# Conditioned recurrence with residual on Trainium2: one product of half B's z moved between half A's products, and one update moved ahead of a transpose

## The chip, the cores and the metric

The kernel runs on one core of a Trainium2 chip. The metric is the device time of one execution in microseconds; the time before is the median of three runs, 1672.14 us (1670.59 to 1672.17).

## What is computed

A gated recurrence over 512 steps of a batch of 8, with 512 inputs and 512 hidden units, and the input added to its output. Cut to what matters:

```python
def step(h, x_t):
    fused = sigmoid(concatenate([x_t, h]) @ w_W + w_b)
    hidden_state, output_state = split(fused, 2)        # r and z below
    memory_state = x_t @ wx_W + wx_b + hidden_state * (h @ wh_W + wh_b)
    h_new = output_state * h + (1.0 - output_state) * tanh(memory_state)
    return h_new, h_new
return x + swapaxes(scan(step, cond, x_by_time), 0, 1)
```

Each step needs the state of the step before in full, so three products with h (for r, z and hh = h @ wh_W + wh_b) and all that follows them lie on a loop through the steps. The products with x do not depend on the state.

## The kernel before

**Layout.** The 512 hidden units are cut into four chunks of 128, the contraction rows of the products. Chunks 0 and 1 are half A of the state (tile `hT` for A, called hTA in the profile), chunks 2 and 3 are half B (hTB). The state is the stationary operand of each product, in 32 columns (8 batch entries for each of 4 steps in a group), and the weights stream past it. The array is used as four column strips of 32 (`128*32` in the profile): the index j of a product picks the strip, and output partitions 32j to 32j+31. In float32 each product shows in the profile as two weight loads and two matmuls, here called two passes.

**Banks.** The outputs of a step lie in three PSUM tiles: `A` (192 columns: hh, z and r of half A), `B` (128 columns: r and hh of half B) and `C` (64 columns: z of half B). There are two sets of them, used in turn by groups of four steps; the x products and biases are put there ahead of time by copies.

**Order on TensorE.** `ORDER` (line 26) is a string, and the loop of lines 349 to 358 issues it in every step but the first (which has `FIRST`). "B0" means: bank B, chunk 0, four products, one for each strip. So A0, A1, B0, B1, C0, C1 read half A's state and A2, A3, B2, B3, C2, C3 read half B's. Behind the twelve items come seven products of the x side for later groups (line 362); the strip of the first product rotates with `turn`, which grows by 7 a step. So three strips get two x products in a step and one gets one, each strip being the short one in every fourth step. The x side runs from step 5 on and issues 62 blocks of 56 products.

**Order on VectorE and ScalarE.** Lines 437 to 462, under a schedule written out by hand: the order of the calls is the order in each engine's queue. For half A: `turn_r(0)` transposes r out of its bank (tr) and ScalarE takes its sigmoid into `md0`; `turn_h(0)` transposes hh into `md1`; `turn_z(0)` transposes z (tz), followed by a sigmoid. `memory(0, q)` is a scan on VectorE that forms the memory state of chunk q, and a tanh on ScalarE. `update(0, q)` is a scan that writes chunk q of the new state of half A. For half B the same follows with index 1: tr, md1 and tz of B stand among the updates of A. Line 446 makes `update(0, 1)` wait for the sigmoid of r of B. Half B's memory scans and updates come last (lines 457 to 460), then two copies of the new state on ScalarE, and small work for later groups.

So A0 of the next step waits for `update(0, 0)`, A1 for `update(0, 1)`, A2 for `update(1, 0)` and A3 for `update(1, 1)`; the transposes of half A wait for the last product of bank A, which is A3's, the transposes tr and md1 of half B for B3, and tz of half B for C3.

Of the kernel before, what the change touches and what calls it, by code (L numbers as in the profile page):

```python
# [22 lines left out]
IDLE = 3  # L23
SYNC = mybir.DependencyInfo(mybir.DependencyClass.Sync, mybir.DependencyReason.DATA)

ORDER = "A0 B0 A1 A2 A3 B1 B2 B3 C0 C1 C2 C3"

FIRST = "A0 x A1 x A2 x A3 B0 B1 B2 B3 C0 C1 C2 C3"

# [11 lines left out]
def tile_cond_rnn_residual(  # L41
# [184 lines left out]
    def act(key, out_, in_, func, **kw):  # L226
        inst = nc.scalar.activation(out_, in_, func, **kw).ins  # L227
        if key in written:
            tc.declare_no_dep(inst, written[key], reason="ordered through VectorE")
        written[key] = inst  # L230
        return inst
# [108 lines left out]
    for i in range(T):  # L340
# [7 lines left out]

        for n in (ORDER if i else FIRST).split():
            if n == "x":  # L350
# [16 lines left out]
        def scan(c_, out_, d0, d1):  # L367

            return nc.vector.tensor_tensor_scan(  # L369
                *[t_[:, :, c_].rearrange("p n c s -> p (n c s)") for t_ in (out_, d0, d1)],  # L370
                0.0,
                ALU.mult,
                ALU.add,
            ).ins
# [8 lines left out]
        def turned(n, hf):  # L383
            t_ = work.tile([P, 2, 32], F32, tag=f"t{n}{hf}", name=f"t{n}{hf}_{i}")
            inst = nc.vector.transpose(t_.rearrange("p c n -> p (c n)"), raw[n][hf]).ins  # L385
            return t_[:, :, rows], inst
# [4 lines left out]
        def turn_r(hf):  # L391
            tr, _ = turned("r", hf)
            r_done[hf] = act(
                ("r", hf, g % 2, s),
                md0[hf][g % 2][:, rows, :, 1].rearrange("p n c -> p c n"),
                tr,
                AF.Sigmoid,
            )

        def turn_h(hf):  # L400
            inst = nc.vector.transpose(  # L401
                md1[hf][g % 2][:, :, :, 0].rearrange("p n c -> p c n"), raw["h"][hf]
            ).ins
            h_done[hf] = inst
            if hf == 0 and i + 1 - NH in pool_done:
                tc.add_manual_dep(inst, pool_done[i + 1 - NH].name, SYNC)

        def turn_z(hf):
            tz, _ = turned("z", hf)
            if hf == 0:  # L410
                inst = nc.vector.memset(idle[:, IDLE - 1 :], 0.0).ins
                tc.add_manual_dep(inst, h_done[0].name, SYNC)
            act(
                ("zc", hf, i % 2),
                hd0[hf][i % 2][:, :, :, 2].rearrange("p n c -> p c n"),
                tz,
                AF.Sigmoid,
                scale=-1.0,
            )
# [6 lines left out]
        def memory(hf, q):  # L426

            c_ = slice(q, q + 1)
            scan(c_, ms[hf], md0[hf][g % 2][:, rows], md1[hf][g % 2][:, rows])
            act(("n", hf, q, i % NH), state(hf, i, 1)[:, :, c_], ms[hf][:, :, c_, 1], AF.Tanh)  # L430

        def update(hf, q):
            s1 = (i + 1) % GS
            new = hT[hf][(i + 1) % NH][:, B * s1 : B * s1 + B]
            return scan(slice(q, q + 1), new, hd0[hf][i % 2], hT[hf][i % NH][:, rows])
# [4 lines left out]
        memory(0, 0)  # L440
        memory(0, 1)
        turn_r(1)
        turn_h(1)
        update(0, 0)
        turn_z(1)
        tc.add_manual_dep(update(0, 1), r_done[1].name, SYNC)
        if i == 0:
# [167 lines left out]
```

## Time and profile before

| what | value |
| --- | --- |
| median of three runs | 1672.14 us (1670.59 to 1672.17) |
| the profiled execution's own time | 1671.53 us |
| its span | 1669.5 us |
| granted TensorE clock | 0.999 |
| steps | 512 |
| busy: PE, weight loads, VectorE, ScalarE, GpSimd | 99%, 98%, 65%, 62%, 18% of the span |

How to read it: PE is TensorE's matmuls, PEld its weight loads, DVE is VectorE, ACT ScalarE, POOL GpSimd. A row of a timeline has the start and the duration in us, the engine, the line of the kernel, the operation, output<-inputs, and how many instructions are merged in it; a bracket gives the idle time of the engine ahead of it and what ended it. The duration of a matmul's record is that of one pass through the array; passes of one strip overlap in the pipeline, so the time from one start to the next is shorter than the duration. A row of the groups ends with busy us, mean ns of one, and the idle time ahead of it. The tile name hTA<-hd0A,hTA is an update of half A, m<-md0B,md1B a memory scan of half B, tr<-B the transpose of r of half B, md1B<-B that of hh, tz<-C that of z.

### The profile page before, as it was taken

What the parts mean: (1) busy time and instruction counts of PE and PEld (TensorE: products, weight loads), DVE (VectorE), ACT (ScalarE), POOL (GpSimd) and SP (SyncE); (2) the same over time, 40 slices, a digit from 0 to 9 for tenths busy, and PEclk for the clock granted to TensorE, in tenths of its full rate; (3) what the DMA queues carried; (4) which work ended last, traced back from release to release, by engine and by line L of the source; (5) the groups of instructions that cost most, each with busy time, mean ns of one, the idle gap of its engine ahead of it and who ended that gap; (6) DMA issues with size and microseconds to landing.
All of it is one profiled execution on the core that took longest, in us unless ns stands there. A gap on an engine that the chain in (4) does not pass through costs nothing.

```text
span 1669.5 us, 130236 instructions
## 1 busy us (share of the span) xinstructions
PE 1658.5 (99%) x56238; PEld 1639.1 (98%) x56238; DVE 1090.2 (65%) x9387; ACT 1029.7 (62%) x5822; POOL 301.7 (18%) x1281
## 2 busy tenths in 40 slices
PE   8999999999999999999999999999999999999998
PEld 5999999999999999999999999999999999999997
DVE  6666666666666666666666666666666666666666
ACT  3666666666666666666666666666666666666665
POOL 1111111111111111111111111111111111111111
PEclk9999999999999999999999999999999999999999
DMA  4000000000000000000000000000000000000000
GB/s 181 11 15 17 15 15 15 17 15 15 14 17 15 15 14 18 14 14 15 18 15 15 14 16 16 15 14 18 15 14 14 18 15 15 15 16 12 10 10 10
DMA packets 37304, 31.43 MB, mean 19 GB/s; under 512 B 4084, under 2 KB 35060, under 8 KB 36600
## 3 DMA queue, kind: packets, MB, share of 16 engines
q1 hardware_dynamic: 36576, 22.95, 4.4%
q8 instruction: 440, 7.21, 1.8%
q14 instruction: 136, 1.11, 0.2%
q10 hardware_dynamic: 152, 0.16, 0.0%
HBM read 14.70 MB, written 8.39 MB: 14 GB/s over the span
## 4 chain that ended last, share of the span: by engine, by line
PE 98%; DVE 1%; DMA 0%; issue 0%; ACT 0%
PE A L199 44%; PE B L199 23%; PE xp L199 20%; PE C L199 12%; DMA rows<-in_bias_dram 0%; DVE tr L385 0%; DVE m L369 0%; DVE tz L385 0%; DVE md1B L401 0%; DVE hTA L369 0%; DVE md1A L401 0%; DVE bias L214 0%; ACT hTB L227 0%; ACT xp L235 0%; DVE rows L131 0%
## 5 line engine op out<-in xcount | busy, mean ns | idle before, releaser
L199 PE MATMUL A<-wa,hTA 128*32 128x192 f32 x8176 | 639.0, 329 | 2.3 <-DVE hTA L369 2.3
L199 PE MATMUL B<-wb,hTA 128*32 128x128 f32 x8192 | 575.2, 273 | 0.0
L199 PE MATMUL A<-wa,hTB 128*32 128x192 f32 x8176 | 508.0, 326 | 0.4 <-DVE hTB L369 0.4
L199 PEld LDWEIGHTS B<-wb,hTA 128*32 128x32 f32 x8192 | 472.9, 122 | 1.1
L385 DVE STREAM_TRANSPOSE tr<-A 128x64 f32<-128x64 f32 x511 | 127.7, 250 | 462.5 <-PE A L199 462.5
L199 PE MATMUL B<-wb,hTB 128*32 128x128 f32 x8192 | 399.5, 273 | 0.0
L199 PEld LDWEIGHTS A<-wa,hTA 128*32 128x32 f32 x8176 | 386.8, 123 | 6.6 <-DVE hTA L369 4.0
L199 PEld LDWEIGHTS A<-wa,hTB 128*32 128x32 f32 x8176 | 373.6, 122 | 2.5 <-DVE hTB L369 0.8
L227 ACT ACTIVATE md0A<-tr 128x16 f32<-128x16 f32 x512 | 112.2, 219 | 419.9 <-DVE tr L385 419.9
L518 POOL TENSOR_TENSOR ot<-xin,hTB 128x16 f32<-128x16 f32 x503 | 125.9, 250 | 1323.4 <-DVE hTB L369 1312.9
L199 PEld LDWEIGHTS B<-wb,hTB 128*32 128x32 f32 x8192 | 322.3, 122 | 0.0
L199 PE MATMUL C<-wb,hTA 128*32 128x64 f32 x8192 | 290.2, 219 | 0.0
L199 PE MATMUL C<-wb,hTB 128*32 128x64 f32 x8192 | 289.7, 220 | 0.1
L199 PEld LDWEIGHTS C<-wb,hTA 128*32 128x32 f32 x8192 | 267.7, 122 | 0.0
L199 PE MATMUL xp<-tw,sx 128*32 128x192 f32 x2976 | 237.5, 326 | 0.0
L199 PEld LDWEIGHTS C<-wb,hTB 128*32 128x32 f32 x8192 | 229.8, 123 | 0.3 <-issue 0.3
L369 DVE TENSOR_TENSOR_SCAN hTB<-hd0B,hTB 128x24 f32<-128x24 f32 x1024 | 157.8, 196 | 100.9 <-ACT hTB L227 99.8
L369 DVE TENSOR_TENSOR_SCAN hTA<-hd0A,hTA 128x24 f32<-128x24 f32 x1024 | 191.9, 187 | 0.0
L199 PE MATMUL xp<-wx,xin 128*32 128x192 f32 (+1 forms) x2048 | 180.9, 331 | 0.0
L227 ACT ACTIVATE hd0B<-tz 128x16 f32<-128x16 f32 x512 | 115.2, 225 | 93.4 <-DVE tz L385 93.4
L227 ACT ACTIVATE hTB<-hTB 128x16 f32<-128x16 f32 x512 | 120.5, 235 | 79.8 <-DVE hTB L369 73.7
L227 ACT ACTIVATE hTB<-m 128x8 f32<-128x8 f32 x1024 | 160.6, 206 | 0.0
(92 smaller groups left out, 2491.0 us busy)
## 6 DMA issues: line engine op xcount, KB each, us to landing
out_dram<-ot SPq DMA_DIRECT2D x128, 64.0 KB, 2.0
xin<-in_x_dram SPq DMA_DIRECT2D x112, 64.0 KB, 2.5
wx<-in_wx_dram SPq DMA_DIRECT2D x4, 768.0 KB, 7.0
wa<-in_wa_dram SPq DMA_DIRECT2D x4, 384.0 KB, 8.9
wb<-in_wb_dram SPq DMA_DIRECT2D x1, 1152.0 KB
xin<-in_x_dram SPq DMA_DIRECT2D x3, 256.0 KB, 8.5
wb<-in_wb_dram SPq DMA_DIRECT2D x1, 384.0 KB, 10.9
head<-in_xh_dram ACTq DMA_DIRECT2D x1, 144.0 KB, 5.0
```

What stands on the lines that cost most here:

```text
L199: nc.tensor.matmul(out_, lhsT, rhs, start=start, stop=False, skip_group_check=True)
L227: inst = nc.scalar.activation(out_, in_, func, **kw).ins
L369: return nc.vector.tensor_tensor_scan(*[t_[:, :, c_].rearrange("p n c s -> p (n c s)") for t_ in (out_, d0, d1)], 0.0, ALU.mult, ALU.add,).ins
L385: inst = nc.vector.transpose(t_.rearrange("p c n -> p (c n)"), raw[n][hf]).ins
L518: return engine.tensor_tensor(ot[:, t, 2 * hf : 2 * hf + 2, :].rearrange("p c n -> p n c"), x_of(c, slice(2 * hf, 2 * hf + 2), t, 1).rearr ...
```

## The change

The order of the products in a step, and the place of one update in VectorE's order:

```diff
-ORDER = "A0 B0 A1 A2 A3 B1 B2 B3 C0 C1 C2 C3"
+ORDER = "A0 C0 A1 A2 A3 B0 B1 B2 B3 C1 C2 C3"
...
         memory(0, 0)
         memory(0, 1)
         turn_r(1)
+        update(0, 0)
         turn_h(1)
-        update(0, 0)
         turn_z(1)
         tc.add_manual_dep(update(0, 1), r_done[1].name, SYNC)
```

C0 (64 columns) takes the place of B0 (128 columns) between A0 and A1, and B0 goes behind A3, ahead of B1. On VectorE the first update of half A goes ahead of the transpose of hh of half B and stays behind the transpose of r of half B. `FIRST`, the order of step 0, stays as it is. Nothing is added and nothing is left out.

## The prediction, made before the change was run

> **What bounds the kernel now.** I read the page first, then the table of waits, then a row of the groups for the period, then one step's timelines on each engine. All times are us from the span's start. The page and its chain of waits:
>
> ```profile
> span 1669.5 us, 130236 instructions
> PE 1658.5 (99%) x56238; PEld 1639.1 (98%) x56238; DVE 1090.2 (65%) x9387; ACT 1029.7 (62%) x5822; POOL 301.7 (18%) x1281
> PE 98%; DVE 1%; DMA 0%; issue 0%; ACT 0%
> ```
>
> TensorE looks saturated, and the waits seem to say so too: VectorE waits for PE, PE hardly for anyone.
>
> ```profile
> DVE tr L385 <- PE A L199: 462.5, 510, 1.4
> DVE hTB L369 <- ACT hTB L227: 99.8, 511, 0.3
> PE A L199 <- DVE hTA L369: 2.3, 10, 0.2
> ```
>
> This is deceptive, because the array is used as four column strips (128*32), so a strip can stand still while PE counts as busy. To see it, work out one strip's work per step and compare it with the period. Period, from the transposes tr<-A (one per step), the window 803 to 1630:
>
> ```profile
> L385 DVE STREAM_TRANSPOSE tr<-A 128x64 f32<-128x64 f32 x257 | 64.2, 250 | 234.1 <-PE A L199 234.1
> 803.09 0.25 DVE L385 STREAM_TRANSPOSE tr<-A 128x64 f32<-128x64 f32 x1 [0.73 <-PE A L199]
> 1630.74 0.25 DVE L385 STREAM_TRANSPOSE tr<-A 128x64 f32<-128x64 f32 x1 [0.73 <-PE A L199]
> ```
>
> (1630.74 - 803.09)/257 = 3.220 a step. Now PE's timeline of one step, where each product is two passes per strip and the first start of a kind is that of the strip that leads:
>
> ```profile
> 802.70 0.27 PE L199 MATMUL B<-wb,hTA 128*32 128x128 f32 x1
> 802.72 0.33 PE L199 MATMUL A<-wa,hTB 128*32 128x192 f32 x1
> ...
> 803.43 0.27 PE L199 MATMUL B<-wb,hTB 128*32 128x128 f32 x1
> ...
> 803.93 0.22 PE L199 MATMUL C<-wb,hTB 128*32 128x64 f32 x1
> ...
> 804.36 0.36 PE L199 MATMUL A<-wa,hTA 128*32 128x192 f32 x1
> ...
> 804.72 0.27 PE L199 MATMUL B<-wb,hTA 128*32 128x128 f32 x1
> ...
> 805.26 0.33 PE L199 MATMUL A<-wa,hTB 128*32 128x192 f32 x1
> ...
> 805.91 0.27 PE L199 MATMUL B<-wb,hTA 128*32 128x128 f32 x1
> ...
> 806.13 0.27 PE L199 MATMUL B<-wb,hTB 128*32 128x128 f32 x1
> ...
> 806.57 0.22 PE L199 MATMUL C<-wb,hTA 128*32 128x64 f32 x1
> ...
> 806.79 0.22 PE L199 MATMUL C<-wb,hTB 128*32 128x64 f32 x1
> ```
>
> A2 and A3 (four passes of 192 columns) take 805.91 - 805.26 = 0.65, or 0.163 a pass; B2 and B3 (four of 128) 806.57 - 806.13 = 0.44, or 0.11; C0 and C1 (four of 64) 806.79 - 806.57 = 0.22, or 0.055. A strip's step has eight of each: 1.30 + 0.88 + 0.44 = 2.62. On top come the seven x products, 192 columns wide like A: three strips take two (0.65), one takes one (0.325), in rotation. So a long strip needs 3.27, a short one 2.945, the mean over four steps is 3.19. The period is 3.22: about 0.02 to 0.03 a step is waiting. Where? At A0: its first record is 0.36 long, not 0.33, so it lay 0.03 to 0.04 in front of its weights. Its weight load, and that of A2:
>
> ```profile
> 804.36 0.28 PEld L199 LDWEIGHTS A<-wa,hTA 128*32 128x32 f32 x7
> 805.16 0.67 PEld L199 LDWEIGHTS A<-wa,hTB 128*32 128x32 f32 x15
> ```
>
> VectorE and one ScalarE row of the same step:
>
> ```profile
> 803.26 0.21 DVE L401 STREAM_TRANSPOSE md1A<-A 128x64 f32<-128x64 f32 x1
> 803.39 0.21 DVE L385 STREAM_TRANSPOSE tz<-A 128x64 f32<-128x64 f32 x1
> ...
> 803.81 0.23 DVE L385 STREAM_TRANSPOSE tr<-B 128x64 f32<-128x64 f32 x1
> 803.96 0.21 DVE L401 STREAM_TRANSPOSE md1B<-B 128x64 f32<-128x64 f32 x1
> 804.09 0.21 DVE L369 TENSOR_TENSOR_SCAN hTA<-hd0A,hTA 128x24 f32<-128x24 f32 x1
> 804.22 0.23 DVE L385 STREAM_TRANSPOSE tz<-C 128x64 f32<-128x64 f32 x1
> 804.37 0.17 DVE L369 TENSOR_TENSOR_SCAN hTA<-hd0A,hTA 128x24 f32<-128x24 f32 x1
> 804.45 0.25 DVE L369 TENSOR_TENSOR_SCAN m<-md0B,md1B 128x16 f32<-128x16 f32 x2
> 804.90 0.31 DVE L369 TENSOR_TENSOR_SCAN hTB<-hd0B,hTB 128x24 f32<-128x24 f32 x2 [0.20 <-ACT hTB L227]
> ```
>
> ```profile
> 804.08 0.22 ACT L227 ACTIVATE md0B<-tr 128x16 f32<-128x16 f32 x1
> ```
>
> The first update of A ends at 804.09 + 0.21 = 804.30, A0's load starts 0.06 later, its multiply at 804.40 (B0 follows at 804.72, two passes on). So a loop binds: end of A3, transposes, sigmoid, scan, tanh, first update, A0. It holds up only the leading strip, the one that had a single x product in the step before. How a lead works: if the last strip never waits, a long strip loses 3.27 - P on it each step, three steps in a row, so P = 3.27 - c/3, where c is the greatest lead that the waits allow. The trace bears it out: the leader's last pass of A3 starts at 802.70 - 0.16 = 802.54, the last strip's at 802.72, c = 0.18, P = 3.21. As a period longer by p also lets the lead grow by p, a wait that comes later by d moves the period by **d/4**: p = (d - p)/3. Without any wait c is 0.244 (three quarters of 0.325) and P is 3.19: 0.02 a step is all that any order can win.
>
> The second loop, that of half B, is nearly as tight. The first update of B starts at 804.90 and ends at about 805.10; A2's load starts at 805.16, and by A0's example its multiply could start 0.04 behind that, at 805.20. It starts at 805.26, when the strip is free. **Slack of A2: 0.06.**
>
> **The change part by part.** No instruction, DMA or wait on a queue of SP or POOL is added or removed; the program's passes and their sizes are the same, so PE's work stays at 3.19.
>
> 1. C0 for B0 between A0 and A1. Two passes of 0.055 stand where two of 0.11 stood: A1, A2 and A3 fall due 0.11 earlier after A0. That helps half A's loop by 0.11 (its wait of about 0.08 at A0 goes) and asks half B's state 0.11 earlier.
>
> 2. B0 behind A3. The end of B3 lies 0.65 behind that of A3 now (803.43 + 0.27 = 803.70 against 802.72 + 0.33 = 803.05). It will lie 0.65 + 0.22 = 0.87 behind A3, and 0.11 later after A0. The transpose tr<-B starts at 803.81, 0.11 behind B3, but tr<-A starts 0.04 behind its A3: so it stands 0.07 in VectorE's queue, and now turns into a wait for PE. It comes 0.11 - 0.07 = 0.04 later after A0. Queued behind it on VectorE are the update of A, the other transposes of B and both memory scans of B.
>
> 3. The update of A ahead of md1B<-B. Now the update starts 804.09 - 803.05 = 1.04 behind the end of A3, held by its tanh; all that leads to the tanh stands ahead of the edit. Behind the change VectorE is free for it at 0.87 + 0.04 + 0.17 (tr<-A to md1A after a wait) = 1.08. With A3 0.11 earlier the update is still 0.07 earlier after A0, and A0's wait nearly or wholly gone. Left behind md1B it would have been some 0.15 later: this part of the change has its use.
>
> 4. VectorE from tr<-B to the memory scan of B. Before: 804.45 - 803.81 = 0.64. After, with the intervals of the rows: tr<-B after a wait 0.17, update 0.08 (as 804.37 to 804.45, since it no longer waits), md1B behind a scan 0.15 (as tz<-C, 804.22 to 804.37), tz<-C behind a transpose 0.13 (as 803.26 to 803.39), second update 0.08: 0.61. The second update also waits for the sigmoid of r of B, by the hand-made dependency: 0.25 + 0.03 + 0.22 + 0.04 = 0.54 behind tr<-B's start, where the queue has it at 0.53; so 0.62. Gain 0.02. If all gaps are at their shortest (0.15, 0.08, 0.13, 0.13, 0.08) it is 0.57, a gain of 0.07; with the widest (0.17, 0.13, 0.15, 0.15, 0.08) 0.68, a loss of 0.04. I take 0.62, nearest to the rows of like neighbours. tz<-C is covered: the passes up to C3 are the same in sum, so C3 still ends at 804.15 against A0, before its turn at 803.85 + 0.40 = 804.25. C0 of the next step must follow tz<-C out of the same bank: that is over at 804.25 + 0.23 = 804.48, before 804.72, where B0 stands now in C0's place.
>
> Sum for A2: due 0.11 earlier, state of B 0.04 - 0.02 = 0.02 later, slack 0.06 used up: late by **0.07** at today's period. The stall goes from A0 to A2, the strip that leads meets it there. Price 0.07/4 = 0.0175 a step. The x products run in 62 x 56/7 = 496 steps (5 to 500): 8.7 us. The first five steps carry equal work on all strips and a longer period, and take nothing. In the last eleven no strip leads, so there the whole 0.07 counts: 0.8 us. These steps:
>
> ```profile
> 1640.09 0.25 DVE L385 STREAM_TRANSPOSE tr<-A 128x64 f32<-128x64 f32 x1 [0.83 <-PE A L199]
> 1643.17 0.25 DVE L385 STREAM_TRANSPOSE tr<-A 128x64 f32<-128x64 f32 x1 [0.83 <-PE A L199]
> ```
>
> At 3.08 they are bound by the loops alone. Together +9.5 on the profiled execution's 1671.5: **1681 us**. (The median shown is 1672.1, 0.6 above that execution, inside the runs' own spread.) Bounds: chain of B at its shortest, late by 0.02: +2.5 and 0.2, 1674; at its widest, 0.13: +16 and 1.4, 1689.
>
> The Trainium skill ("TensorE: Matmul & The Clock Gate", Part 3, "The mechanism") says that matmuls start and end strictly in program order. The rows differ on column strips: B1 on hTA starts at 802.70, before the last pass of A3 at 802.72, which precedes it in the program. By that rule no strip could lead, and A2's 0.07 would be paid whole.
>
> **Rivals.**
> (a) Faster. A2 isn't late, and the wait at A0 goes: P = 3.19, 496 x 0.02 = -10, and -1.2 in the last eleven steps (A's loop is shorter by 0.11): 1660. For it: A0's wait binds today, and the update is put ahead just where it counts. Against it: half B's state would have to come 0.13 to 0.15 sooner than summed; it decides from 0.07 sooner on, and B3's end alone rules most of that out.
> (b) No difference: PE's work sets the time, and a wait shifts from A0 to A2 at the same price, 1671.5. For it: PEld at 98%. Against it: 0.02 a step of waiting is seen, and A2's slack is smaller than the shift. The Trainium skill ("Perfetto Trace Analysis", "Identifying the Most-Contended Engine") judges TensorE's headroom by the busy share of weight loads; by its 98% here the time would stay. The strips show that this share hides waits of one strip.
> (c) Slower than forecast: a late load of A2 needs 0.10 to its multiply (805.16 to 805.26) instead of A0's 0.04. Late by 0.13: 0.0325 x 496 + 1.4 = +17.5, 1689.
> (d) A late A2 holds all four strips: 0.07 x 507 = +35, 1707. Against it: A0's wait of 0.08 today costs 0.02.
>
> **Chances and range.** Forecast 0.66 (own range 1674 to 1688), (a) 0.11, (b) 0.11, (c) 0.09, (d) 0.03. A measurement of this kernel tells about 0.2%, 3.3 us, from no change. Faster 0.11; same 0.13, which is (b) and the forecast's lowest edge; slower 0.76. Range 1669 to 1690: it leaves out (a), (d) and the edges.
>
> **What would show it.** Right: A0's first record 0.33 long again, A2's first 0.03 to 0.04 longer than 0.33 and its load 0.06 behind the first update of B; a new wait of tr<-B for PE's B bank, about 0.15 x 511 = 75 us in all (0.91 behind A3 against 0.76, where the queue would be free); the period at 3.235; the last eleven steps at about 3.15; tr<-B to the memory scan 0.62. Wrong: no such wait at A2 and a period of 3.19 or 3.20; or tr<-B not later after A0; or a period up by the whole of A2's lateness.

## The result, and the profile after

The changed kernel takes 1683.41 us (median of 6 runs, 1683.32 to 1684.51) against 1671.6 for the kernel before on the same chip: a ratio of 1.0074, 95% interval 1.0061 to 1.0087. The profiled execution took 1683.32. Its page and two rows of its waits, to be read beside those of before:

```profile
span 1681.4 us, 130236 instructions
PE 1670.4 (99%) x56238; PEld 1618.1 (96%) x56238; DVE 1142.7 (68%) x9387; ACT 1092.2 (65%) x5822; POOL 303.1 (18%) x1281
```

```profile
DVE tr L385 <- PE A L199: 390.0, 510, 1.1
DVE hTB L369 <- ACT hTB L227: 100.0, 511, 0.3
```

PE is still at 99%; nothing on the page says why the span grew by 11.9 us. The weight loads' share fell from 98 to 96%, and VectorE waits less for bank A (390 against 462). The step shows it. VectorE's timeline of one step of the changed kernel, and the one ScalarE row that matters, the sigmoid of r of half B:

```profile
802.42 0.25 DVE L385 STREAM_TRANSPOSE tr<-A 128x64 f32<-128x64 f32 x1 [0.84 <-PE A L199]
...
802.96 0.28 DVE L369 TENSOR_TENSOR_SCAN m<-md0A,md1A 128x16 f32<-128x16 f32 x2
803.30 0.25 DVE L385 STREAM_TRANSPOSE tr<-B 128x64 f32<-128x64 f32 x1
803.47 0.17 DVE L369 TENSOR_TENSOR_SCAN hTA<-hd0A,hTA 128x24 f32<-128x24 f32 x1
803.56 0.23 DVE L401 STREAM_TRANSPOSE md1B<-B 128x64 f32<-128x64 f32 x1
803.70 0.20 DVE L385 STREAM_TRANSPOSE tz<-C 128x64 f32<-128x64 f32 x1
803.83 0.20 DVE L369 TENSOR_TENSOR_SCAN hTA<-hd0A,hTA 128x24 f32<-128x24 f32 x1
803.96 0.25 DVE L369 TENSOR_TENSOR_SCAN m<-md0B,md1B 128x16 f32<-128x16 f32 x2
804.40 0.31 DVE L369 TENSOR_TENSOR_SCAN hTB<-hd0B,hTB 128x24 f32<-128x24 f32 x2 [0.19 <-ACT hTB L227]
```

```profile
803.58 0.22 ACT L227 ACTIVATE md0B<-tr 128x16 f32<-128x16 f32 x1
```

The transpose tr<-B now starts 803.30 - 802.42 = 0.88 behind tr<-A; before it was 803.81 - 803.09 = 0.72. (In the median of 473 steps it is 0.87 against 0.73.) The update of A follows it at 0.17, as summed. The second update of A starts at 803.83, 0.03 behind the end of the sigmoid (803.58 + 0.22 = 803.80), is 0.20 long instead of 0.17, and half B's memory scan comes 0.13 behind it, not 0.08. From tr<-B to that scan it is 0.66; 0.64 before, 0.62 in the prediction.

TensorE in the same step: the matmuls at A0, C0 and A2, and the weight load of A2.

```profile
803.76 0.33 PE L199 MATMUL A<-wa,hTA 128*32 128x192 f32 x1
...
804.08 0.22 PE L199 MATMUL C<-wb,hTA 128*32 128x64 f32 x1
```

```profile
804.66 0.37 PE L199 MATMUL A<-wa,hTB 128*32 128x192 f32 x1
```

```profile
804.66 0.58 PEld L199 LDWEIGHTS A<-wa,hTB 128*32 128x32 f32 x16
```

A0's first record is 0.33 long and C0 follows two passes on, at 0.32: the wait at A0 is gone. A2's load starts at 804.66, 0.05 behind the end of half B's first update (804.40 + 0.21), and its first matmul record is 0.37 long, like A0's in the kernel before. With its operands there it would have started at 803.76 + 0.325 + 0.11 + 0.325 = 804.52; it multiplies at 804.70. **The wait has moved from A0 to A2 and become longer.**

Read as the mark of a wait, the longer record also tells how many strips wait. Over 483 steps from the middle of the kernel before, the first A0 record of a step is over 0.338 long in 480, a later strip's in 2 at most, and the first A2 record in 1. In the changed kernel the first A0 record is that long in 2, the first A2 record in 479, a later strip's in 5 at most. In the last ten steps of either kernel all four strips wait: before at A0 alone, in the changed kernel at A0 and at A2. So one strip, the leader, waits while there are x products, and all four once there are none.

The period, from twelve steps that nothing disturbs, and from the last eleven steps:

```profile
782.98 0.25 DVE L385 STREAM_TRANSPOSE tr<-A 128x64 f32<-128x64 f32 x1 [0.57 <-PE A L199]
...
821.81 0.25 DVE L385 STREAM_TRANSPOSE tr<-A 128x64 f32<-128x64 f32 x1 [0.81 <-PE A L199]
...
1657.39 0.25 DVE L385 STREAM_TRANSPOSE tr<-A 128x64 f32<-128x64 f32 x1 [0.77 <-PE A L199]
1660.57 0.25 DVE L385 STREAM_TRANSPOSE tr<-A 128x64 f32<-128x64 f32 x1 [0.77 <-PE A L199]
```

(821.81 - 782.98)/12 = 3.236 a step, and 1660.57 - 1657.39 = 3.18 in the last steps, where it was 3.08. So the steps with x products lost 0.024 each and the last eleven 0.10: 496 x 0.024 + 11 x 0.10 = 13 us. The span grew by 11.9. Of the difference 1.1 is single steps off the usual length, which every execution has: they add 2.5 us in the profiled execution of before and 1.4 in this one.

### The profile page after: what moved, and what is told of

Same layout as the page of the kernel before. It is cut to its first block, busy times and chain, and to the rows that moved or that the text cites. A ratio compares the mean times of both kernels' runs of the same rounds, so it can differ in the third digit from the quotient of the medians.

```text
span 1681.4 us, 130236 instructions
## 1 busy us (share of the span) xinstructions
PE 1670.4 (99%) x56238; PEld 1618.1 (96%) x56238; DVE 1142.7 (68%) x9387; ACT 1092.2 (65%) x5822; POOL 303.1 (18%) x1281
## 4 chain that ended last, share of the span: by engine, by line
PE 98%; DMA 1%; DVE 0%; ACT 0%; issue 0%; SPq 0%
PE A L199 41%; PE B L199 26%; PE xp L199 19%; PE C L199 13%; DMA wb<-in_wb_dram 1%; DMA wx<-in_wx_dram 0%; DVE tr L385 0%; DVE hTA L369 0%; ACT hTB L227 0%; ACT xp L235 0%; DVE hTB L369 0%; SPq L136 0%; DVE tz L385 0%; DVE md1B L401 0%; ACT hd0B L227 0%
## 5 line engine op out<-in xcount | busy, mean ns | idle before, releaser
L199 PE MATMUL C<-wb,hTA 128*32 128x64 f32 x8192 | 477.2, 219 | 0.0
L199 PEld LDWEIGHTS A<-wa,hTA 128*32 128x32 f32 x8176 | 434.2, 122 | 6.4 <-DVE hTA L369 3.1
L199 PEld LDWEIGHTS C<-wb,hTA 128*32 128x32 f32 x8192 | 436.1, 122 | 1.6
L199 PE MATMUL B<-wb,hTA 128*32 128x128 f32 x8192 | 359.2, 273 | 0.7 <-DMA wb<-in_wb_dram 0.7
L199 PE MATMUL B<-wb,hTB 128*32 128x128 f32 x8192 | 359.3, 273 | 0.1
L199 PEld LDWEIGHTS A<-wa,hTB 128*32 128x32 f32 x8176 | 301.9, 123 | 33.6 <-DVE hTB L369 4.4
L199 PEld LDWEIGHTS B<-wb,hTA 128*32 128x32 f32 x8192 | 308.6, 122 | 1.9 <-DMA wb<-in_wb_dram 1.1
L199 PEld LDWEIGHTS B<-wb,hTB 128*32 128x32 f32 x8192 | 281.9, 122 | 0.3 <-DMA wb<-in_wb_dram 0.3
L199 PE MATMUL C<-wb,hTB 128*32 128x64 f32 x8192 | 249.8, 219 | 0.0
L199 PEld LDWEIGHTS C<-wb,hTB 128*32 128x32 f32 x8192 | 199.8, 122 | 0.0
```

The costliest lines, as they stand in the source:

```text
L199: nc.tensor.matmul(out_, lhsT, rhs, start=start, stop=False, skip_group_check=True)
```

## The experiments

The later runs came in three groups, each on one chip beside runs of the kernel before. Single long steps are far more frequent in them, and the times scatter (the kernel before: 1676 to 1698 us). So the runs are compared by two numbers that such steps do not touch, worked out from the starts of tr<-A: **steps** is the median over all stretches of twelve steps that hold none longer than 3.26 (3.28 for before and before_pad, no limit for after_pad_long), **end** the median of the first eight of the last eleven (over all eleven it differs by 0.003 at most). The lateness is the time by which half B's state comes too late for A2. At the end of the program all four strips wait, so by the theory it is paid whole there and can be read off: end less 3.078, the end of the kernel before.

| kernel | steps | more than before | end | more than before | a quarter of that | ratio of times, 95% interval |
| --- | --- | --- | --- | --- | --- | --- |
| before | 3.212 | | 3.078 | | | |
| changed | 3.236 | 0.024 | 3.181 | 0.103 | 0.026 | 1.0074, 1.0061 to 1.0087 |
| update_alone | 3.226 | 0.015 | 3.140 | 0.062 | 0.015 | 1.0038, 1.0023 to 1.0053 |
| order_alone | 3.236 | 0.024 | 3.181 | 0.103 | 0.026 | 1.0053, 1.0037 to 1.0070 |
| no_dep | 3.227 | 0.015 | 3.139 | 0.061 | 0.015 | 1.0032, 1.0022 to 1.0042 |
| scan_first | 3.227 | 0.015 | 3.141 | 0.063 | 0.016 | 1.0034, 1.0019 to 1.0049 |
| scan_first_fill | 3.214 | 0.003 | 3.091 | 0.013 | 0.003 | 0.9995, 0.9979 to 1.0011 |
| before_pad | 3.213 | 0.001 | 3.085 | 0.007 | 0.002 | 1.0020, 0.9997 to 1.0044 |
| after_pad | 3.254 | 0.042 | 3.249 | 0.171 | 0.043 | 1.0074, 1.0049 to 1.0099 |
| after_pad_long | 3.550 | 0.339 | 3.550 | 0.472 | 0.118 | 1.09 (one run) |
| leader_swap | 3.211 | 0.000 | 3.092 | 0.014 | 0.003 | 0.9999, 0.9985 to 1.0014 |

The fourth and the sixth column are the test of the theory, since they come from different steps of an execution. They agree within 0.003 in every row but that of the long pad, up to a lateness of 0.17. The diffs below are against the changed kernel, if nothing else is said.

### One part of the change alone

The update's move alone, with the products in the old order:

```diff
-ORDER = "A0 C0 A1 A2 A3 B0 B1 B2 B3 C1 C2 C3"
+ORDER = "A0 B0 A1 A2 A3 B1 B2 B3 C0 C1 C2 C3"
```

> Products in the order of before, update of A ahead of the transpose md1B. Theory (half B's state late for A2, paid by a quarter through the leading strip): the update waits for its tanh as before, at 0.28 behind the start of tr<-B, so md1B, tz<-C and B's memory scan come about 0.13 later; less the slack of 0.06 that leaves 0.07, so 0.0175 a step for 496 steps and 0.07 for the last 11: 1671.6 + 9.5 = 1681 us. Rival 1 (the short product C0 between A0 and A1 costs TensorE itself, by weight loads that no longer hide): 1671.6, no change. Rival 2 (a late A2 holds all strips): 1671.6 + 35 = 1707.

Ratio 1.0038, steps 3.226 and end 3.140: 0.015 a step and 0.062, where 0.0175 and 0.07 were expected. Both rivals, no change and 35 us more, lie outside the interval. VectorE's rows of one step show how an update put ahead makes everything behind it late:

```profile
784.13 0.23 DVE L385 STREAM_TRANSPOSE tr<-B 128x64 f32<-128x64 f32 x1
784.41 0.21 DVE L369 TENSOR_TENSOR_SCAN hTA<-hd0A,hTA 128x24 f32<-128x24 f32 x1
784.54 0.22 DVE L401 STREAM_TRANSPOSE md1B<-B 128x64 f32<-128x64 f32 x1
...
784.90 0.25 DVE L369 TENSOR_TENSOR_SCAN m<-md0B,md1B 128x16 f32<-128x16 f32 x2
```

The update still starts 0.28 behind tr<-B, where its tanh lets it, and the queue behind it waits with it: from tr<-B to the memory scan 0.77 instead of 0.64. Of these 0.13 the end of the program shows 0.062; the other 0.07 was slack at A2. This part costs time by itself, and no step got shorter by it.

The order alone, with the update where it was:

```diff
+        turn_h(1)
         update(0, 0)
-        turn_h(1)
```

> Products in the new order, update of A where it was, behind md1B. Theory: B's memory scan stays bound by the sigmoid of r of B, so half B's state comes as late as in the changed kernel; the update of A comes 0.13 later and makes the leading strip wait about 0.11 at A0, but that strip waits 0.18 at A2 anyway, so nothing is added: 1683 us within 2. Rival (the update's place matters, as the prediction's third point says): the wait at A0 is added, 0.11/4 x 496 = 14, so 1697.

Steps 3.236, end 3.181, the same as the changed kernel to the third digit; the ratio of 1.0053 has an interval that overlaps the changed kernel's. Here A0 waits again, and it costs nothing:

```profile
932.91 0.36 PE L199 MATMUL A<-wa,hTA 128*32 128x192 f32 x1
```

The leading strip loses there what it would otherwise lose at A2: its A2 starts 0.84 behind its A0 in the median, in the changed kernel 0.91. With the new order of products neither steps nor end show an effect of the update's place.

### The chain on VectorE that the prediction had too short

```diff
-        tc.add_manual_dep(update(0, 1), r_done[1].name, SYNC)
+        update(0, 1)
```

> The changed kernel without the hand-made wait of the second update of A for the sigmoid of r of B. Theory: in the changed kernel the update starts 0.037 behind that sigmoid's end, so it waits, and a scan that waited holds the queue 0.12 instead of 0.09; without the wait B's memory scan starts 0.03 sooner: 0.03/4 x 496 + 0.3 = 4 less, 1679 us. Rival: the wait only moves to the memory scan, which needs that sigmoid itself: 1683.

Steps 3.227 and end 3.139, 0.009 and 0.042 less than the changed kernel; 0.03/4 was expected, 0.0075. The second update no longer waits, is 0.17 long, and the scan follows at once:

```profile
800.57 0.25 DVE L385 STREAM_TRANSPOSE tr<-B 128x64 f32<-128x64 f32 x1
...
801.10 0.17 DVE L369 TENSOR_TENSOR_SCAN hTA<-hd0A,hTA 128x24 f32<-128x24 f32 x1
801.19 0.27 DVE L369 TENSOR_TENSOR_SCAN m<-md0B,md1B 128x16 f32<-128x16 f32 x2
```

From tr<-B to the scan it is 0.62; the prediction's sum without the wait was 0.61. So the wait for the sigmoid in the second update is the part of the lateness that the prediction missed.

```diff
-        tc.add_manual_dep(update(0, 1), r_done[1].name, SYNC)
+        memory(1, 0)
+        update(0, 1)
 ...
-        memory(1, 0)
         memory(1, 1)
```

> The changed kernel with the first memory scan of B ahead of the second update of A, without the hand-made wait. Theory: the scan starts at the sigmoid's end, 0.12 sooner than in the changed kernel, and half B's state with it; the update comes 0.1 later, which the leading strip's wait at A2 covers. 0.03 x 496 + 1.2 = 16 less than 1683.4: 1667 us, faster than before. Rival 1 (the order of the products itself costs TensorE): 1683. Rival 2 (A1, which now waits for the later update, takes the stall over): 1675 to 1680.

The expectation failed: 3.227, no better than no_dep, and 1687 us. VectorE's and ScalarE's rows:

```profile
800.71 0.21 DVE L385 STREAM_TRANSPOSE tz<-C 128x64 f32<-128x64 f32 x1
800.89 0.19 DVE L369 TENSOR_TENSOR_SCAN m<-md0B,md1B 128x16 f32<-128x16 f32 x1
801.00 0.18 DVE L369 TENSOR_TENSOR_SCAN hTA<-hd0A,hTA 128x24 f32<-128x24 f32 x1
```

```profile
800.58 0.22 ACT L227 ACTIVATE md0B<-tr 128x16 f32<-128x16 f32 x1
```

The sigmoid ends at 800.80, the scan starts at 800.89, 0.09 later and not 0.04, and is 0.19 long instead of 0.16 in no_dep. So in the median its start is 0.035 sooner behind tr<-B than in no_dep, its end 0.004, and half B's first update starts at 1.06 or 1.07 in both. In front of the scan the trace has an instruction of VectorE's sequencer that only waits (800.83 to 800.85), on the semaphore that VectorE itself counts up, 0.04 behind the end of md1B. The scan needs a result of ScalarE and one of VectorE's own, and the second wait got an instruction of its own. A memset of one column that waits for md1B takes its place in the next kernel (against scan_first):

```diff
+        fill = nc.vector.memset(idle[:, IDLE - 1 :], 0.0).ins
+        tc.add_manual_dep(fill, h_done[1].name, SYNC)
         memory(1, 0)
         update(0, 1)
```

> The kernel scan_first with a memset of one column that waits for the transpose md1B, put ahead of half B's first memory scan. In scan_first that scan started 0.09 behind the end of the sigmoid of r of B, not 0.04, behind an instruction on VectorE that waits for md1B alone. Theory: the memset takes that wait along and is over before the sigmoid, so the scan starts about 0.05 sooner and half B's state with it: the last eleven steps from 3.141 to 3.09, the steps from 3.228 to 3.215, 6 us less than scan_first, within 3 us of before. Rival (the scan's start is bound by the sigmoid alone): no change against scan_first.

Steps 3.214, end 3.091, ratio 0.9995: the products of the changed kernel at the time of the kernel before. The scan now starts 0.55 behind tr<-B (863.16 - 862.61) and 0.04 behind the sigmoid (862.90 + 0.22 = 863.12):

```profile
862.61 0.25 DVE L385 STREAM_TRANSPOSE tr<-B 128x64 f32<-128x64 f32 x1
...
863.16 0.19 DVE L369 TENSOR_TENSOR_SCAN m<-md0B,md1B 128x16 f32<-128x16 f32 x1
```

```profile
862.90 0.22 ACT L227 ACTIVATE md0B<-tr 128x16 f32<-128x16 f32 x1
```

So all but 0.003 of the 0.024 a step lies in when half B's state is ready, not in the order of the products as TensorE sees it.

### The price of lateness, measured by adding some

One more memset on VectorE ahead of half B's memory scans, in the kernel before and in the changed one:

```diff
+    pad = const.tile([P, 96], F32, name="pad")
 ...
+        nc.vector.memset(pad, 0.0)
         memory(1, 0)
         memory(1, 1)
```

> The kernel before with one more VectorE memset of 96 columns ahead of half B's first memory scan; from the memsets of the trace (59 ns for 1 column, 98 for 48, 165 for 128) it holds the queue about 0.09. Theory: half B's state comes 0.09 later, 0.06 of it is slack at A2, the rest 0.03 is paid by a quarter: steps from 3.211 (mean of four, undisturbed) to 3.218, the last eleven from 3.078 to about 3.105; 4 us more than before. Rival (no slack, half B is on the loop as half A is): 3.233 and 3.17, 12 us more. Rival (VectorE has time to spare): nothing.

> The changed kernel with the same memset at the same place. Theory: no slack is left at A2, so 0.09 is paid by a quarter in the steps and whole in the last eleven: steps from 3.236 to 3.258, the last eleven from 3.181 to 3.27; 12 us more than the changed kernel's 1.0074, a ratio of about 1.015. Rival (a late A2 holds all strips): 0.09 x 507 = 46 more, ratio 1.035.

The pad was worth 0.07, not 0.09: from tr<-B to half B's first update it is 1.153 with it and 1.084 without in the kernel before, 1.175 and 1.105 in the changed one (medians). In the kernel before it costs 0.001 a step and 0.007 at the end: the slack at A2 is 0.06 to 0.07, and it takes nearly all of the pad. In the changed kernel, where no slack is left, the same pad costs 0.018 a step, a quarter of 0.07, and 0.068 at the end, all of it:

```profile
1082.47 0.25 DVE L386 STREAM_TRANSPOSE tr<-A 128x64 f32<-128x64 f32 x1 [0.54 <-PE A L200]
...
1121.51 0.25 DVE L386 STREAM_TRANSPOSE tr<-A 128x64 f32<-128x64 f32 x1 [0.77 <-PE A L200]
...
1681.49 0.25 DVE L386 STREAM_TRANSPOSE tr<-A 128x64 f32<-128x64 f32 x1 [0.77 <-PE A L200]
1684.73 0.25 DVE L386 STREAM_TRANSPOSE tr<-A 128x64 f32<-128x64 f32 x1 [0.77 <-PE A L200]
```

(1121.51 - 1082.47)/12 = 3.253; 1684.73 - 1681.49 = 3.24 (the median is 3.249). The ratio of times, 1.0074, was expected at 1.015. The smaller pad explains about 0.002 of the difference. In the third group the changed kernel itself comes to 1.0050 only (below), and the long steps blur the rest; the undisturbed steps are the firmer reading.

> The changed kernel with a memset of 384 columns there, about 0.33 of queue. Theory: the quarter holds only while a strip leads; the lead is used up when the period reaches the long strip's work of 3.27, that is 0.15 later than in the changed kernel, and the other 0.18 is paid whole: steps of 3.45, the last eleven 3.51; 109 more than the changed kernel, ratio about 1.07. Rival (a quarter throughout): 3.318, 41 more. Rival (whole throughout): 3.566, 165 more.

```profile
943.19 0.25 DVE L386 STREAM_TRANSPOSE tr<-A 128x64 f32<-128x64 f32 x1 [0.53 <-PE A L200]
...
985.79 0.25 DVE L386 STREAM_TRANSPOSE tr<-A 128x64 f32<-128x64 f32 x1 [0.77 <-PE A L200]
```

This pad was worth 0.367 (1.473 - 1.105). Steps and end are now the same, (985.79 - 943.19)/12 = 3.55: no strip leads any more. The pad costs 0.314 a step, all of the 0.367 but the 0.055 by which the changed kernel's steps lay above its end. "A quarter throughout" would be 3.33 and is refuted, and so is the whole price throughout, 3.60. With the pad's real size the expectation's sum gives 3.27 + (0.367 - 0.15) = 3.49, 0.06 too little. It let the lead end too late. The end column is the loop of half B by itself, and no step can be shorter than that loop. In the changed kernel it is 3.181, so it reaches the long strip's 3.27 with 0.09 more lateness, not with 0.15; beyond that the period is the loop: 3.181 + 0.367 = 3.548, and 3.550 is measured in both columns. The records agree: in this kernel the first A2 record of all four strips is longer in each of the 483 steps, in the changed kernel that of one strip.

### An order for each strip, and the two kernels once more

Against scan_first_fill:

```diff
+            swap = {"B0": "C", "C0": "B"}.get(n) if 6 <= i <= 500 else None
-            for j in range(NQ):
-                j = (j + turn[0]) % NQ
+            for first_j in range(NQ):
+                j = (first_j + turn[0]) % NQ
+                bank = swap if swap and first_j == 0 else n[0]
```

> scan_first_fill with one thing more: in steps 6 to 500 the strip that leads (first in the step's rotation) takes B0 between A0 and A1 and C0 behind A3, as before, and the three others take C0 there and B0 behind A3, as in the changed kernel. Theory: the end of A3 is that of the last strip, so half A's loop keeps the 0.11 it won; the strip that leads needs half B's state 0.11 later again, so it no longer waits at A2, and the others lead by less. Then no wait is left that holds a strip: steps at 3.193, the work of the strips alone being 3.19, against 3.211 before; the last eleven as in scan_first_fill, 3.09. 496 x 0.018 = 9 less than before: ratio 0.995. Rival (the place of the products costs TensorE, whatever the strip): as scan_first_fill, 3.213 and 1.000. Rival (products out of step between strips block one another in the order of issue): slower than before.

The wait at A2 is gone (the leader's first matmul of A2 starts 0.868 behind that of A0 in the median, the work of A0, B0 and A1 and no more), and yet most steps are as long as before: 3.211, with a tenth of all four-step means at 3.194 or less. The ratio is 0.9999, so the expected gain did not come. The trace points at the expectation's second rival, that products out of step block one another in the order of issue. The weight loads of one step, where three strips are ahead of the fourth:

```profile
668.93 0.12 PEld L199 LDWEIGHTS B<-wb,hTB 128*32 128x32 f32 x1
668.94 0.13 PEld L199 LDWEIGHTS C<-wb,hTB 128*32 128x32 f32 x2
```

The first row is the fourth strip's last load of B3, the second the first loads of C2 of two others, two items further on in the order. In 290 of 483 steps from the middle the first load of C2 starts 2 to 6 ns behind the last one of B3, and never ahead of it. In the changed kernel it is that close in 3 steps and 160 ns behind in the median. The C2 and C3 records that are longer than usual by over 12 ns, the mark of a wait, number 704 of 7728 here, 9 in the changed kernel and 167 in the kernel before. What these waits cost in the period wasn't isolated. No version that beats the kernel before was found.

> The changed kernel once more, on the chip of these runs. Theory and rivals alike: steps of 3.236 where nothing disturbs them, ratio 1.0074 within the interval measured.

> The kernel before, profiled on the chip of these runs. If the longer times of this chip come from it and not from the edits: steps of 3.211 where nothing disturbs them, and single steps much longer, with PE waiting for nothing that the profile shows, more of them than on the first chip.

Steps of 3.236 and 3.212, as in the first profiles; the ratio of the changed kernel is 1.0050 here, interval 1.0033 to 1.0067. The kernel before has 25 steps over 3.3 here, of the 493 from step 7 on, against 7 in its first profile. Rows of its waits in which PE's queues wait for nothing that the profile shows:

```profile
PEld xp L199 <- issue: 8.2, 29, 0.6
PEld C L199 <- issue: 1.8, 5, 0.6
```

In its first profile the first of these rows had 7.3 us in 24 waits, the second 0.3 us, once. So the longer and more scattered times do not come from the edits, though these rows name only a part of them. The expectation's "ratio 1.0074 within the interval measured" was missed by a little. The two profiled executions differ by 12.3 us (1690.69 and 1678.40), the medians of all runs by 7.3; why the kernel before scatters more here isn't shown.

## Why the prediction was right, point by point

**What bounds the kernel.** Right. The lead of a strip and the price of a quarter are shown: in the table steps and end agree as 1 to 4, and a long pad ends that price. PE's 98 or 99% hid it in all of them.

**C0 for B0 (part 1).** Right: A0's wait went, A2's came. **B0 behind A3 (part 2).** Right: in the median tr<-B starts 0.145 later behind tr<-A, as 0.11 earlier and 0.04 later after A0 make it (0.15). But the announced row of 75 us for tr<-B waiting for bank B is not in the table of waits: the idle time is counted from the end of the record in front, not from when the queue is free, so the wait shows as 803.30 - (802.96 + 0.28) = 0.06 only, too short for that table.

**The update ahead (part 3).** The timing was right (0.17 behind tr<-B, A0 no longer waits), its worth was not: "this part of the change has its use" falls with order_alone, 3.236 with it and without it. A wait of the leading strip at A0 is free as long as it waits longer at A2.

**VectorE's chain (part 4): the term that was mis-sized.** 0.62 was summed and 0.66 measured. The sum had the tie between queue and sigmoid (0.53 against 0.54) and allowed 0.01 for it; it left out that a scan which waits holds the queue 0.13 and not 0.08. The prediction's own rows show that 0.13 (804.09 to 804.22, the first update, which waits for its tanh), and it used it for that update alone, in its widest case. no_dep, without that wait, has 0.62.

**The sum.** Late by 0.07 at A2 was predicted, 0.10 is read at the end of the program. With 0.66 for 0.62 the prediction's sum would be 0.11 + 0.04 + 0.02 - 0.06 = 0.11. 0.10/4 x 496 + 0.10 x 11 = 13.5 instead of 9.5; measured 11.8 between the medians. The slack of 0.06 is borne out by before_pad and update_alone (0.06 and 0.07). Two hits are partly luck. The announced period of 3.235 was met by 3.236, but the prediction started from 3.220, a mean with the long steps in it: undisturbed it is 3.212, and the rise is 0.024, not 0.0175. And the time came within 2.4 us of the 1681 although the steps lost 3.5 to 4 us more than summed, since the single long steps happened to add 1.1 us less. The last eleven steps came to 3.18, not 3.15, by the same mis-sized term.

**Rivals.** (a) needed half B's state sooner; it came later. (b), an equal price, and with it the judgement by the weight loads' 98%, is refuted by the ratio of 1.0074. (c) is refuted by A2's rows: load at 804.66, multiply at 804.70 (the record is 0.04 longer), so 0.04 and not 0.10. (d) is refuted by after_pad: 0.018 a step for 0.07. So the rule of the Trainium skill that matmuls keep the order of the program ("TensorE: Matmul & The Clock Gate", Part 3, "The mechanism") does not describe the column strips here: B1 on hTA started at 802.70, ahead of A3's last pass at 802.72, and that lead is what makes the price.

## What to carry to other kernels

Where an array is split into strips with uneven work, look for the strip that leads: a busy share of 99% says nothing of it, and a wait costs only the leader's share (here a quarter) until the loop that waits is as long as the longest strip's work, then all of it. Before moving a product ahead to shorten one loop, ask which operand falls due sooner by it, and how much slack that one has. Stretches of the same execution with and without the spare work (here the last eleven steps) give the lateness and its price separately, and they are steadier than the times of runs.

## What was not expected of the hardware

A scan on VectorE that had to wait for ScalarE holds the queue longer: 0.20 long and 0.13 to the next, against 0.17 and 0.08 or 0.09 without a wait, in otherwise equal instructions. Where it needs results of two engines, it started 0.09 behind the later one, and 0.04 behind it once another instruction had taken one of the waits. In the medians half B's first update came 0.04 sooner without the first (no_dep) and 0.05 sooner without the second (scan_first_fill), beside the 0.10 by which the changed kernel is late.
